# A graph kernel on Trainium2: the sums of the first 32 nodes, instead of 16, from a bf16 matrix of counts

## The chip, the cores and the metric

The kernel runs on one core of a Trainium2 chip. The metric is the device time of one execution in microseconds (us); the median of the runs shown is quoted, and lower is better. Engines are named as in the profile: PE is TensorE's matmul, PEld its weight load, DVE VectorE, ACT ScalarE, POOL GpSimd, SP SyncE. "L516" is line 516 of the kernel before.

## What is computed

There are 6250 nodes with 256 features each and 100,000 edges, each with a source `src`, a destination `dst` and one of 8 types. The edges are sorted by `dst`, and `dst` grows with the square of the edge's place: node 0 has many edges, late nodes have few. Three layers of a relational graph convolution come first, then an attention layer; both have a residual and a layer norm. The part that matters here is the layer:

```python
for l in range(n_layers):                       # 3 layers
    xr = jnp.einsum('nd,rde->rne', x, W_rel[l]) # 8 types
    msg = xr[edge_type, src]
    agg = jax.ops.segment_sum(msg, dst, num_segments=x.shape[0])
    x = jax.nn.relu(agg + x @ W_root[l] + bias[l])
...
x = _layernorm(x + L0(x))
x = _layernorm(x + L1(x))                       # the attention layer
```

All is float32.

## The kernel before

**Sums first, weights later.** For each destination and each type the kernel sums the rows `x[src]` over the edges, and multiplies the sums by the weights of the type afterwards. The 100,000 edges are cut into 782 tiles of 128. An edge tile is handled so: POOL fetches its 128 rows by an indirect DMA (`gather`, L495, one DMA for each tile, L499); DVE makes a 128 x 8W matrix of zeros and ones that tells destination and type of each edge (`onehot`, L479, for four tiles at once, four steps ahead); PE multiplies rows and matrix (`windows`, L504, matmuls L516, two fp32 matmuls for each tile); DVE adds the result, a window of W destinations (3 to 26, growing along the edges), to the sums S in SBUF (`add`, L521, L528). S is a ring of 4 or of 3 node tiles, one ring for the late edges (f = 0, "A") and one for the earlier ones (f = 1, "B").

**Dense work.** When all edges of a node tile are through, `dense` (L577) multiplies its sums by the weights: 16 fp32 matmuls of 256 columns (L586), and two for the root weights (L582). They are handed out in pieces of one matmul, six pieces a step (PIECE), so that they lie between the windows. `finish` (L598) adds the bias on DVE, ACT takes the relu, SP stores the rows for the next layer; ACT clears the ring's columns (`clear`, L594).

**Steps and their order.** `Plan.order()` puts the tiles into groups of four, from the last edges to the first, A and B groups by turns. A layer goes through the 188 groups, one a step, and the code order within a step (L785 to L830) is the order in which every engine's queue gets its instructions: preparation of the attention (last layer, from step PREP_AT = 164), two moves of `counting`, one of `hot`, loads of node rows, the gathers of this step, the onehots of the fourth step ahead, logits, `finish`, the windows, dense pieces, the additions, transposes and folds. All engines take their instructions in order. The order is written out by hand (`tc.manual_schedule`), so nothing is rearranged.

**The first nodes.** The edges of the first nodes are not gathered at all. For HOT = 16 nodes the plan leaves out the first 36 tiles (`TH`). In their place stands a matrix A of counts: how often each source row is used by each pair of one of 16 nodes and one of 8 types, 128 columns for each of the 49 row tiles. `count` (L640) makes it once, in layer 0, from step COUNT_AT = 56: for each pair of node and edge tile, 138 in all, DVE makes a 128 x 392 matrix of zeros and ones in bf16 (L654), and PE multiplies it (L663) with another (L649); ACT copies the result into A, in fp32 (L666). `products` (L670) then computes, in every layer from step HOT_AT = 130, A times the rows: SP loads four row tiles at a time (512 KB) into a buffer "msg", PE multiplies in fp32 (L692), a step later, and DVE adds to `sums` (L697); at the end two transposes bring the sums into S. 13 such loads take 26 steps.

**Buffers.** The gathered groups and the rows for `products` share the pool `mp` of 8 buffers "msg" (L205), used in turn. The PSUM pool `ps_w` has 4 buffers for windows, `ps_d` has 2, for dense results, counts and products; `ps_t` has 1. The pool `hp` (L208), one for all layers, holds the tiles of `count`, `products` and `prepare`.

**A flag.** `tables` counts cases in which the plan's assumptions on the edges don't hold; if there are any, a general kernel runs behind the fast one (L154). It does not run with these inputs.

Of the kernel before, what the change touches and what calls it, by code (L numbers as in the profile page):

```python
# [10 lines left out]
F32 = mybir.dt.float32  # L11
# [9 lines left out]
P = 128  # L21
# [2 lines left out]
NS = (4, 3)  # L24
PAD = 32
MARGIN = 800
HOT = 16
SELS = 6
LOWS = 17
COUNT_AT = 56  # L30
HOT_AT = 130
NEAR = 450
DB = 32
PREP_AT = 164
# [83 lines left out]
@with_exitstack  # L118
def kernel(
    ctx: ExitStack,  # L120
    tc: tile.TileContext,
    x: bass.AP,
    src: bass.AP,
    dst: bass.AP,
    edge_type: bass.AP,
    w_rel: bass.AP,
    w_root: bass.AP,
    bias: bass.AP,
    weight: bass.AP,
    attn_l: bass.AP,  # L130
    attn_r: bass.AP,
    out: bass.AP,
):
# [12 lines left out]
    dram = ctx.enter_context(tc.tile_pool(name="dram", bufs=1, space=DRAM))  # L146
    xs = [x] + [dram.tile([N, D], F32, name=f"x{l}") for l in range(1, L)]

    flag = const.tile([1, 1], I32, name="flag")

    fast(tc, const, pl, x, xs, src, dst, edge_type, w_rel, w_root, bias, weight,
         attn_l, attn_r, out, flag)

    bad = nc.values_load(flag[0:1, 0:1], min_val=0, max_val=6 * T)  # L154
    with tc.If(bad > 0):
        general(tc, x, src, dst, edge_type, w_rel, w_root, bias, weight, attn_l, attn_r, out)


def fast(tc, const, pl, x, xs, src, dst, edge_type, w_rel, w_root, bias, weight,
# [10 lines left out]
    with ExitStack() as top:  # L170
# [14 lines left out]
        yT0 = tab.tile([P, KC, P], F32, name="yT0")  # L185


        A = tab.tile([P, NT, HOT * R], F32, name="A")

        psi = top.enter_context(tc.tile_pool(name="psi", bufs=1, space=PSUM))  # L190
        iota = psi.tile([P, max(R * WMAX, NT * R)], F32, name="iota")
# [10 lines left out]
        with ExitStack() as s:  # L202
# [2 lines left out]
            mp = s.enter_context(tc.tile_pool(name="mp", bufs=8))  # L205
            op = s.enter_context(tc.tile_pool(name="op", bufs=AHEAD + 2))
            xp = s.enter_context(tc.tile_pool(name="xp", bufs=3))
            hp = s.enter_context(tc.tile_pool(name="hp", bufs=1))  # L208
            ps_w = s.enter_context(tc.tile_pool(name="ps_w", bufs=4, space=PSUM))
            ps_d = s.enter_context(tc.tile_pool(name="ps_d", bufs=2, space=PSUM))  # L210
            ps_t = s.enter_context(tc.tile_pool(name="ps_t", bufs=1, space=PSUM))
# [30 lines left out]
            with tc.manual_schedule():  # L242
                for l in range(L):
                    wr, wo = load_w(l)
                    opn = layer(
                        tc, pl, l, l == L - 1, groups, ready, S, hold, A, hk, hl, idx, key, pos,
                        iota, ident, wr, wo, bias_b, x, xs, eps, w1x, altab, y,
                        (al3, ga, hif, yT0, lane, dst, iota_p),
                        mp, op, xp, hp, ps_w, ps_d, ps_t, H)
# [211 lines left out]


def layer(tc, pl, l, final, groups, ready, S, hold, A, hk, hl, idx, key, pos, iota, ident, wr, wo,
          bias_b, x, xs, eps, w1x, altab, y, att, mp, op, xp, hp, ps_w, ps_d, ps_t, H):
    nc = tc.nc
    N, D = x.shape
    KC = D // P
# [172 lines left out]
    def count():  # L640

        lows, made, pc = {}, [], None
        pairs = [(n, t) for n in range(HOT) for t in pl.hot_tiles(n)]
        for m in range(len(pairs) + SELS - 2):
            if m < len(pairs):
# [24 lines left out]
    def products():  # L670

# [26 lines left out]
        pt = ps_t.tile([P, 4 * P], F32, name="pt")  # L698
        for k in range(KC):
            nc.tensor.transpose(pt[:, k * P:(k + 1) * P], sums[:, k * P:(k + 1) * P], ident)  # L700
        for k in range(KC):
            o = cols(1, 0)[:, k * R:(k + 1) * R, :HOT]
            nc.vector.tensor_tensor(
                o, o, pt[:, k * P:k * P + HOT * R].rearrange("p (n r) -> p r n", r=R), ALU.add)
        yield

    al3, ga, hif, yT0, lane, dst, iota_p = att
# [77 lines left out]
    for i in range(NG + 5):  # L785
# [592 lines left out]
```

## Time and profile before

| | |
|---|---|
| median of 3 runs | 2970.67 us (2969.94 to 2975.62) |
| the profiled execution | 2981.72 us, span 2980.0 us |
| granted PE clock, mean | 0.939 |
| PE / PEld busy | 2684.0 us (90%) / 2436.3 us (82%) |
| POOL busy | 2136.6 us (72%) |
| DVE / ACT busy | 1664.3 us (56%) / 452.7 us (15%) |
| gathers (L499) | 2238, 0.95 us each |
| matmul instructions of windows (L516) / dense (L586) | 8952 / 4800 |
| first and last gather begin, layer 0 | 11.3, 945.4 us |
| first and last gather begin, layers 1 and 2 | 964.8, 2866.8 us |

An fp32 matmul shows as two MATMUL instructions. In the groups, the number after the bar is the busy time, then the mean duration in ns of one instruction, which for PE contains the time in the pipeline, so that instructions follow each other faster than their duration. "Idle before" is the time that the engine stood still ahead of them, with what ended it.

### The profile page before, as it was taken

Reading aid. Unit: us, or ns where it says so; the run is one execution under the profiler, and the core shown is the slowest. Engines: PE = TensorE matmul, PEld = TensorE weight load, DVE = VectorE, ACT = ScalarE, POOL = GpSimd, SP = SyncE. Lnnn points to the kernel's source line nnn. Section 1 sums busy time; section 2 is a strip of 40 time slices with the busy share of each in tenths; the row PEclk is TensorE's granted clock in tenths of the full one; section 3 lists DMA queues with packets and bytes.
Section 4 is the critical chain, followed back from the end, with each engine's and each line's share of the span. In section 5 each row is a group of like instructions: output and inputs, shape, how many; then the busy total and the mean of one; then the engine's idle time right before and its main releaser. Section 6 shows DMA issues by size and latency. Waiting matters only on the chain.

```text
span 2980.0 us, 45437 instructions
## 1 busy us (share of the span) xinstructions
PE 2684.0 (90%) x15806; PEld 2436.3 (82%) x15807; DVE 1664.3 (56%) x4097; ACT 452.7 (15%) x599; POOL 2136.6 (72%) x2254
## 2 busy tenths in 40 slices
PE   5999999999877899998988987789999999999985
PEld 4998888888776788988877887678888888888874
DVE  7555677764432555555454443355556655554768
ACT  2111111111001011111111010111111111110114
POOL 6777777777775777777777777577777777777731
PEclk9999999999988899999999997799999999998985
DMA  4444444445433444444444544344444444454534
GB/s 151 122 124 123 122 120 123 120 133 159 146 116 106 129 123 122 124 124 117 123 117 148 163 126 117 118 123 127 130 124 128 124 125 128 136 176 137 167 114 167
DMA packets 203054, 388.99 MB, mean 131 GB/s; under 512 B 42885, under 2 KB 128004, under 8 KB 202820
## 3 DMA queue, kind: packets, MB, share of 16 engines
q0 software_dynamic: 107424, 293.48, 34.2%
q1 hardware_dynamic: 92200, 89.76, 9.4%
q8 instruction: 131, 2.15, 0.3%
q10 hardware_dynamic: 3196, 2.76, 0.3%
q14 instruction: 103, 0.84, 0.1%
HBM read 360.18 MB, written 25.65 MB: 129 GB/s over the span
## 4 chain that ended last, share of the span: by engine, by line
PE 70%; POOL 10%; issue 8%; DVE 6%; DMA 3%; ACT 2%; DVEq 0%; ACTq 0%; POOLq 0%; SPq 0%
PE pw L516 31%; PE pd L586 31%; POOL msg L499 10%; PE pd L582 4%; DMA msg<-x,idx 2%; DVE S L528 2%; PE pd L692 1%; PE pt L560 1%; PE pt L636 1%; ACT xT L563 1%; DMA msg<-in_x_dram,idx 1%; PE pd L663 1%; DVE st L1034 0%; DVE z L1022 0%; PE pw L749 0%
## 5 line engine op out<-in xcount | busy, mean ns | idle before, releaser
L499 POOL DMA_INDIRECT msg<-x,idx x1492 | 1417.2, 950 | 504.3 <-issue 420.2
L516 PE MATMUL pw<-oh,msg 128*128 128x160 f32 (+22 forms) x8952 | 1300.7, 302 | 187.4 <-DMA msg<-x,idx 95.2
L528 DVE TENSOR_TENSOR S<-S,pw 128x320 f32 (+22 forms) x2238 | 904.3, 404 | 989.5 <-PE pd L586 504.3
L516 PEld LDWEIGHTS pw<-oh,msg 128*128 128x128 f32 x8952 | 1245.0, 201 | 253.6 <-issue 109.6
L586 PE MATMUL pd<-wr,S 128*128 128x256 f32 x4800 | 1130.9, 386 | 2.2 <-DVE S L528 1.9
L586 PEld LDWEIGHTS pd<-wr,S 128*128 128x128 f32 x4800 | 913.2, 194 | 122.6 <-DVE S L528 3.9
L499 POOL DMA_INDIRECT msg<-in_x_dram,idx x746 | 708.0, 949 | 236.4 <-issue 209.7
L483 DVE TENSOR_TENSOR oh<-iota,key 128x640 f32<-128x640 f32 (+23 forms) x564 | 363.9, 647 | 25.6 <-issue 13.9
L595 ACT ACTIVATE S<-S 128x2048 uint32<-128x2048 uint32 x150 | 285.0, 1900 | 25.9 <-PE pd L586 25.9
L563 ACT COPY xT<-pt 128x256 f32<-128x256 f32 x195 | 72.4, 371 | 1048.1 <-PE pt L560 1046.7
L609 ACT ACTIVATE h<-pd 128x256 f32<-128x256 f32 x98 | 37.7, 385 | 903.3 <-DVE pd L606 669.0
L582 PE MATMUL pd<-wo,xT 128*128 128x256 f32 x588 | 167.8, 411 | 3.2 <-ACT h L609 3.2
L606 DVE TENSOR_TENSOR pd<-pd,bias_b 128x256 f32<-128x256 f32 x147 | 63.2, 430 | 186.6 <-PE pd L586 186.4
L582 PEld LDWEIGHTS pd<-wo,xT 128*128 128x128 f32 x588 | 109.3, 203 | 12.9 <-ACT h L609 3.6
L654 DVE TENSOR_SCALAR sel<-iota,hk 128x392 bf16<-128x392 f32 x138 | 80.4, 613 | 0.0
L619 ACT ACTIVATE rs<-mv,eps 128x1 f32<-128x1 f32 x49 | 14.4, 295 | 403.8 <-DVE mv L618 403.8
L692 PE MATMUL pd<-msg,A 128*128 128x256 f32 x294 | 71.9, 387 | 1.9 <-DMA msg<-x 1.9
L692 PEld LDWEIGHTS pd<-msg,A 128*128 128x128 f32 x294 | 55.6, 196 | 9.1 <-issue 2.2
L560 PE MATMUL pt<-ident,xin 128*128 128x128 f32 x294 | 58.3, 281 | 1.4 <-ACT xT L563 1.4
L636 PEld LDWEIGHTS pt<-w1x,xT 128*128 128x128 f32 x192 | 26.6, 201 | 35.3 <-ACT xT L563 35.3
L560 PEld LDWEIGHTS pt<-ident,xin 128*128 128x128 f32 x294 | 41.8, 147 | 13.2 <-ACT xT L563 2.8
L636 PE MATMUL pt<-w1x,xT 128*128 128x4 f32 x192 | 30.8, 266 | 23.6 <-ACT xT L563 23.6
(187 smaller groups left out, 629.3 us busy)
## 6 DMA issues: line engine op xcount, KB each, us to landing
msg<-x,idx POOLq DMA_INDIRECT x1492, 2.8
x<-h SPq DMA_DIRECT2D x96, 128.0 KB
xin<-x SPq DMA_DIRECT2D x96, 128.0 KB
msg<-x SPq DMA_DIRECT2D x24, 512.0 KB
msg<-in_x_dram,idx POOLq DMA_INDIRECT x746, 2.8
y<-yt SPq DMA_DIRECT2D x49, 128.0 KB
xin<-in_x_dram SPq DMA_DIRECT2D x48, 128.0 KB
msg<-in_x_dram SPq DMA_DIRECT2D x12, 512.0 KB
```

What stands on the lines that cost most here:

```text
L483: nc.vector.tensor_tensor(oh[:, :len(g), :w], iota[:, :w].unsqueeze(1).to_broadcast([P, len(g), w]), key[:, g[0]:g[-1] + 1].unsqueeze(2).t ...
L499: nc.gpsimd.indirect_dma_start(out=msg[:, q, :], out_offset=None, in_=table, in_offset=bass.IndirectOffsetOnAxis(ap=idx[:, t:t + 1], axis=0))
L516: nc.tensor.matmul(pw[:, k * w:(k + 1) * w], msg[:, q, k * P:(k + 1) * P], oh[:, q, :w], start=True, stop=True)
L528: ins = nc.vector.tensor_tensor(o, o, pw.rearrange("p (a b) -> p a b", b=W), ALU.add)
L560: nc.tensor.transpose(pt[:, k * P:(k + 1) * P], t[:, k * P:(k + 1) * P], ident)
L563: nc.scalar.copy(xT.rearrange("p k n -> p (k n)"), pt[:, :D])
L582: nc.tensor.matmul(pd[:, :D], xT[:, k], wo[:, k], start=(k == 0), stop=False)
L586: i = nc.tensor.matmul(pd[:, :D], s[:, k * R + r], wr[:, k, r], start=(xT is None and k == r == 0), stop=(k == KC - 1 and r == R - 1))
L595: i = nc.scalar.memzero(cols(f, j))
L636: nc.tensor.matmul(pt[:, :H], yT[:, k], w1x[:, k, D + H:D + 2 * H], start=(k == 0), stop=(k == KC - 1))
L654: nc.vector.tensor_scalar(oh, iota[:, :NT * R], float(512 * n), hk[:, t:t + 1], op0=ALU.add, op1=ALU.is_equal)
L692: nc.tensor.matmul(ph[:, :D], A[:, j], t[:, n], start=(n == 0), stop=(j == js[-1]))
```

## The change

HOT becomes 32, so the plan leaves out 52 tiles instead of 36 and a layer has 184 groups instead of 188; there are 272 pairs of node and edge tile instead of 138. A has 256 columns for each row tile, in bf16, which takes as many bytes as before. Counts up to 256 are exact in bf16; a new check takes the largest count and raises the flag if it is over 256. Counting begins at step 8 instead of 56. `products` begins at step 148 in layer 0 and 130 in the others. It loads one load further ahead, splits the fp32 rows into three bf16 parts whose sum is exact (ACT copies the first, DVE subtracts it in place, ACT copies the second, and in the next step DVE makes the third), and multiplies each of them with both halves of A: six bf16 matmuls for each row tile instead of one in fp32. The sums have two halves of 256 columns. The pool `hp` is made anew for each layer.

```diff
-HOT = 16
+HOT = 32
...
-COUNT_AT = 56
-HOT_AT = 130
+COUNT_AT = 8
+HOT_AT = 148, 130
...
-    bad = nc.values_load(flag[0:1, 0:1], min_val=0, max_val=6 * T)
+    bad = nc.values_load(flag[0:1, 0:1], min_val=0, max_val=6 * T + P)
...
-        A = tab.tile([P, NT, HOT * R], F32, name="A")
+        A = tab.tile([P, NT, HOT * R], BF16, name="A")
...
-            hp = s.enter_context(tc.tile_pool(name="hp", bufs=1))
...
-                    opn = layer(
...
+                    with tc.tile_pool(name=f"hp{l}", bufs=1) as hp:
+                        opn = layer(
...
     def count():
         lows, made, pc = {}, [], None
+        top = hp.tile([P, HOT], F32, name="top")
...
                 if t == tiles[-1]:
                     nc.scalar.copy(A[:, :, n * R:(n + 1) * R],
                                    pc[:, :NT * R].rearrange("p (j r) -> p j r", r=R))
+                    nc.vector.tensor_reduce(top[:, n:n + 1], pc[:, :NT * R], AX.X, ALU.max)
             yield
+
+        most = hp.tile([P, 2], F32, name="most")
+        nc.vector.tensor_reduce(most[:, 0:1], top, AX.X, ALU.max)
+        nc.vector.tensor_scalar(most[:, 0:1], most[:, 0:1], 256.5, None, op0=ALU.is_gt)
+        nc.vector.memset(most[:, 1:2], 1.0)
+        pt = ps_t.tile([P, 4 * P], F32, name="pt")
+        nc.tensor.matmul(pt[0:1, 0:1], most[:, 0:1], most[:, 1:2], start=True, stop=True)
+        nc.vector.tensor_copy(most[0:1, 0:1], flag)
+        nc.vector.tensor_tensor(most[0:1, 0:1], most[0:1, 0:1], pt[0:1, 0:1], ALU.add)
+        nc.vector.tensor_copy(flag, most[0:1, 0:1])
+        yield
...
-        sums = hp.tile([P, D], F32, name="sums")
-        for js in loads:
-            t = load(js)
+        HH = HOT * R // P
+        HN = HOT // HH
+        sums = hp.tile([P, HH * D], F32, name="sums")
+        x3 = hp.tile([P, 3, GT * D], BF16, name="x3")
+        rows_of, ph, m = {0: load(loads[0])}, None, 0
+        yield
+        for m, js in enumerate(loads):
+
+            if m + 1 < len(loads):
+                rows_of[m + 1] = load(loads[m + 1])
+            w = len(js) * D
+            t = rows_of.pop(m).rearrange("p a d -> p (a d)")[:, :w]
+            nc.scalar.copy(x3[:, 0, :w], t)
+            nc.vector.tensor_tensor(t, t, x3[:, 0, :w], ALU.subtract)
+            nc.scalar.copy(x3[:, 1, :w], t)
             yield
+            nc.vector.tensor_tensor(x3[:, 2, :w], t, x3[:, 1, :w], ALU.subtract)
             ph = ps_d.tile([P, 512], F32, name="pd")
-            for n, j in enumerate(js):
-                nc.tensor.matmul(ph[:, :D], A[:, j], t[:, n], start=(n == 0), stop=(j == js[-1]))
+            for h in range(HH):
+                for n, j in enumerate(js):
+                    for c in range(3):
+                        nc.tensor.matmul(ph[:, h * D:(h + 1) * D], A[:, j, h * P:(h + 1) * P],
+                                         x3[:, c, n * D:(n + 1) * D], start=(n == c == 0),
+                                         stop=(j == js[-1] and c == 2))
             yield
-            if js[0] == 0:
-                nc.vector.tensor_copy(sums, ph[:, :D])
+            if m == 0:
+                nc.vector.tensor_copy(sums, ph[:, :HH * D])
             else:
-                nc.vector.tensor_tensor(sums, sums, ph[:, :D], ALU.add)
+                nc.vector.tensor_tensor(sums, sums, ph[:, :HH * D], ALU.add)
...
-        if i >= HOT_AT:
+        if i >= HOT_AT[min(l, 1)]:
             next(hot, None)
...
-    v = A.rearrange("p j s -> p (j s)").bitcast(BF16)
+    v = A.rearrange("p j s -> p (j s)")
```

Four transposes instead of two, and four additions instead of two, bring the sums into S at the end of `products`.

More of the change, by code (lines that the diff above doesn't have):

```diff
@@ L244, in fast @@
                     wr, wo = load_w(l)
-                    opn = layer(
[L246 to L249, printed above, removed]
+                    with tc.tile_pool(name=f"hp{l}", bufs=1) as hp:
+                        opn = layer(
+                            tc, pl, l, l == L - 1, groups, ready, S, hold, A, hk, hl, idx, key, pos,
+                            iota, ident, wr, wo, bias_b, x, xs, eps, w1x, altab, y,
+                            (al3, ga, hif, yT0, lane, dst, iota_p), flag,
+                            mp, op, xp, hp, ps_w, ps_d, ps_t, H)
         with tc.manual_schedule():
@@ L463, in layer @@
 def layer(tc, pl, l, final, groups, ready, S, hold, A, hk, hl, idx, key, pos, iota, ident, wr, wo,
-          bias_b, x, xs, eps, w1x, altab, y, att, mp, op, xp, hp, ps_w, ps_d, ps_t, H):
+          bias_b, x, xs, eps, w1x, altab, y, att, flag, mp, op, xp, hp, ps_w, ps_d, ps_t, H):
     nc = tc.nc
@@ L693, in products @@
             yield
-            if js[0] == 0:
-                nc.vector.tensor_copy(sums, ph[:, :D])
+            if m == 0:
+                nc.vector.tensor_copy(sums, ph[:, :HH * D])
             else:
-                nc.vector.tensor_tensor(sums, sums, ph[:, :D], ALU.add)
+                nc.vector.tensor_tensor(sums, sums, ph[:, :HH * D], ALU.add)
         pt = ps_t.tile([P, 4 * P], F32, name="pt")
+        for h in range(HH):
+            for k in range(KC):
+                nc.tensor.transpose(pt[:, (h * KC + k) * P:(h * KC + k + 1) * P],
+                                    sums[:, h * D + k * P:h * D + (k + 1) * P], ident)
@@ L699, in products @@
         for k in range(KC):
[L700 to L704, printed above, removed]
+            for h in range(HH):
+                o = cols(1, 0)[:, k * R:(k + 1) * R, h * HN:(h + 1) * HN]
+                q = (h * KC + k) * P
+                nc.vector.tensor_tensor(
+                    o, o, pt[:, q:q + P].rearrange("p (n r) -> p r n", r=R), ALU.add)
```

## Prediction

> **What bounds the kernel now.** I read the chain of waits first, then the costliest groups, then busy time by stretch, then the waits of POOL and VectorE, and last the timeline inside single steps.
>
> ```profile
> PE 70%; POOL 10%; issue 8%; DVE 6%; DMA 3%; ACT 2%; DVEq 0%; ACTq 0%; POOLq 0%; SPq 0%
> L499 POOL DMA_INDIRECT msg<-x,idx x1492 | 1417.2, 950 | 504.3 <-issue 420.2
> ```
>
> The chain names PE, but POOL is as full: a gather is busy 0.95 us and followed by 0.30 us of "issue", 1.25 us in all, and 746 of them per layer make 934 us of a layer's some 950. So two engines run side by side with nearly equal loads. Busy time by stretch, one for each layer (stretch, then PE, PEld, DVE, ACT, POOL, clock, DMA):
>
> ```profile
> 40.00:350.00 310.00, 296.07 (x1702) 271.37 (x1702) 180.63 (x363) 55.53 (x59) 234.73 (x248) 0.98 0.43 126
> 990.00:1280.00 290.00, 279.96 (x1614) 256.56 (x1613) 157.78 (x311) 45.58 (x53) 219.53 (x232) 0.99 0.42 122
> 2000.00:2270.00 270.00, 256.93 (x1500) 232.66 (x1499) 163.59 (x370) 48.17 (x68) 200.53 (x212) 0.99 0.44 128
> ```
>
> 310 us hold 248 gathers (1.25 us each): POOL never stops in layers 0 and 1. In layer 2 it is 212 in 270 us (1.27): there it waits.
>
> To see who leads I paired, in the timeline, the 4 gathers of each step with its 16 matmuls of L516, and took as **lag** the time from the end of the step's last gather to its first matmul. At least 1.9 us of it is the landing. Layer 0: 14.7 at step 8, 23.7 at step 56, 28.2 at step 80, 5.8 at 128, then 2 to 8. Layer 1: 1.9 at step 8, 11.7 at 44, 1.9 at 130, 9.3 at 140, 6.1 at the end. Layer 2: 3.8, 30.4 at 44, 38.0 at 60, 20.0 at 130, 18.0 at the end, never back at the floor. So layers 0 and 1 end with POOL as the bound, and layer 2 is PE's from step 12 on. 38 us is where 8 msg buffers are full and POOL has to wait for PE.
>
> ```profile
> POOL msg L499 <- PE pw L516: 43.3, 108, 3.5
> DVE S L528 <- PE pd L586: 504.3, 105, 7.7
> DVE S L528 <- PE pw L516: 375.6, 296, 8.9
> ```
>
> The second line matters below: in 105 of the some 560 steps the additions into S (L528) cannot start when the windows are done, but only when PE has ended that step's dense matmuls, which read S. One such step in the timeline (start, duration, what, and in brackets the idle time before it):
>
> ```profile
> 2662.92 2.75 PE L586 MATMUL pd<-wr,S 128*128 128x256 f32 x12
> 2665.71 1.92 DVE L528 TENSOR_TENSOR S<-S,pw 128x288 f32 x4 [4.50 <-PE pd L586]
> ```
>
> DVE stands idle for 4.5 us, and starts its four additions when the 12 dense matmuls are over.
>
> [...] For 392 columns [...] the trace has 165 (a pair of L663 takes 0.33 us to the next instruction). For 256 columns [...] I use 0.11 us. [...] the trace has 693 ns for 512 columns at L569[...]. [...] the gathers around it mostly keep 1.25 us, a few are up to 0.4 us late. The new subtractions are of that kind too, 78 of them: 0 to 15 us of POOL time, 0 taken, because POOL waits in that phase anyway.
>
> **The change part by part.** Unit times: a 256-column fp32 matmul instruction 0.219 us (12 in 2.63 on the chain; each fp32 matmul is two instructions), a window instruction 0.128 below 128 columns, 0.15 to 0.17 above (16 in 2.71 at 208), a count 0.165. I went through the steps in the order of the plan and summed windows, dense pieces, transposes, counts and products of each stretch. That reproduces what is seen where PE has no lack of data: layer 0, steps 8 to 56, 254 us worked out, 250 seen (66.6 to 316.2 us).
>
> *Gathers removed.* Tiles 0 to 35 are left out now; the limit for 32 nodes gives 52. 16 gathers per layer at 1.25 us are **-20 us** of POOL per layer, -60 in all. PE loses 16 x 4 x 0.128 = -8.2 us per layer. Groups fall from 188 to 184 a layer, while dense work stays, so it is packed 2% tighter.
>
> *Counting, layer 0.* Pairs of node and tile go from 138 to 272: +134 x 0.165 = +22 us PE, +134 x 0.613 (L654) = +82 us DVE, and they start at step 8 instead of 56, exactly where PE is 96% busy. PE work for steps 8 to 56 becomes 266 us (250 seen + 96 x 0.165) against POOL's 48 x 5.006 = 240: lag 14.7 + 26 = 40, over the limit of 38; POOL waits 2. Steps 56 to 80: 126 against 120, 6 more. Then PE is faster (80 to 148: 314 against 340), lag about 9 at step 148. The 32 new maxima make DVE wait for PE's counts ahead of its own onehots, and the pd buffer held by a count is now held among denser dense work; nothing before shows this: 0 to 15 us (half a microsecond for each maximum), I take 5, since in steps 56 to 127 the same pd sharing shows no excess over the sum. The final flag chain, the memset and the copies: one small chain, 0 to 2, in the 5.
>
> *Products.* Per row tile 6 bf16 matmuls x 0.11 instead of 2 instructions x 0.219: 147 x 0.22 = +32 us PE, 10.8 per layer. ACT gets 26 copies of 1024 columns per layer (about 0.97 us each from L595, 1900 ns for 2048), hidden: ACT is 15% busy. DVE gets 26 subtractions x 1.22 and additions of 512 columns instead of 256: some +35 us per layer, hidden as load (DVE is 45% busy there) but **not as a chain**. Today PE's products wait for a load alone. Then the 24 matmuls of a product wait for the third part, a subtraction that DVE makes after the previous step's additions. If that step had dense work without conflict, DVE is through in its shade: 0. If it had none (13 of the 28 steps, since five dense tiles fall due there and each takes three), PE stands for the last addition and the subtraction: about 1.6 us. If the additions waited for the dense part (19%): four additions, say 1.7, + 1.22 + 0.2 = 3.1. Mean 0.46 x 1.6 + 0.19 x 3.1 = **1.33 us per product, 17 per layer**. Bounds 0 and 3.1; below nothing is excluded, because PE's own work per product grows too.
>
> *The msg buffers.* A product's rows also take one of the 8. Today PE frees them one step after the load; then they are loaded one step earlier and freed by DVE three steps after. Every second step's gather must then wait for work of the step but two before it: three steps of 5.0 less 4.0 (windows, last addition, subtraction) and less the 4.9 of its own gathers leave a lag of at most 6 us in these 28 steps. A hint from before: in layer 2 the lag falls from 20 to 13 in the product phase, with POOL waits of up to 2 us.
>
> Sums for the product phase (28 steps, POOL 140.2): PE 137 in layer 0 and 139 in layer 1, 154 and 156 with the chain.
> Layer 0: POOL -20 + 2 + 6 + 3 (lag 9 pressed to 6) + 14 + 5 = **+10**.
> Layer 1: -20 + (156 - 140 - 4 of lag that is free) = **-8**.
> Layer 2, PE's: -8.2 + 10.8 + 17, four steps' small stalls -1.6, and the preparation, whose last two rounds fall behind the last gather instead of one, +2: **+20**. Its 20 us of POOL only lengthen a wait.
> Total +22. The profiled execution took 2981.7 (span 2980.0), so 3003.7 against it; the runs' median is 2970.67, 0.4% lower, and I forecast **2993**.
>
> **Rivals.** *A, faster: DVE is always ahead, the products cost matmuls alone.* Layer 0: -20 + 2 + 6 + 3 = -9, layer 1: -20 (139 fits into 140), layer 2: +3. That is -26: 2945. For it: DVE is only half busy; against it, the 504 us of L528. The break-even is at 0.75 us of chain per product (39 x 0.75 = 29): below that the kernel is faster. Chance 0.17. *B, no change*: 0.6 to 0.9 us per product, 2971. Chance 0.14. *C, much slower*: every product pays the long wait of 3.1 us, 40 a layer: layer 0 -20 + 11 + 37 + 5 = +33, layer 1 -20 + 39 - 4 = +15, layer 2 +3 + 40 = +43; 3062. Dense work in the half of the steps that hides the chain speaks against it. Chance 0.10. *D, gathers bound everything*: -60, 2911; the lag in layer 2 speaks against it. Chance 0.03. The forecast, up to 3015: 0.56.
>
> About 0.2%, 6 us, is what a measurement can tell from no change. Faster 0.20 (A and D), same 0.14, slower 0.66. The range 2945 to 3035 leaves out D, part of A and most of C.
>
> **What would show it.** In the profile after: 2190 gathers; 272 counts; bf16 products of 256 columns at 0.11 us; PE waiting on DVE's third part, some 1.3 us each; POOL waiting for PE in layer 0 before step 80 and in every product phase; first gathers of layers 1 and 2 some 10 us late and 2 us late. I am wrong if PE's wait for the third part is below 0.75 us, if POOL runs on at 1.25 us through the product phases, or if layer 2 shortens with its gathers.

## The result, and the profile after

The changed kernel takes **3087.78 us** (median of 4 runs, 3083.85 to 3089.36) against 2971.5 us for the kernel before in the same rounds: a ratio of 1.0387, 95% interval 1.0369 to 1.0405. The forecast was slower, by 22 us; it is slower by 116. The profiled execution has a span of 3086.5 us (before: 2980.0) and a mean granted clock of 0.936 (0.939).

The chain of waits of this run breaks off after a tenth of the span, so I lean on the groups, the waits and the stretches instead. First some of the costliest groups of the changed kernel:

```profile
L499 POOL DMA_INDIRECT msg<-x,idx x1460 | 1407.1, 964 | 573.2 <-issue 411.1
L720 PE MATMUL pd<-x,A 128*128 128x256 bf16 x882 | 137.8, 317 | 75.0 <-DVE x L715 61.3
L664 PE MATMUL pd<-sel,low 128*128 128x392 bf16 x272 | 69.2, 331 | 18.6 <-DVE top L669 18.6
L711 ACT CAST x<-msg 128x1024 bf16<-128x1024 f32 (+1 forms) x39 | 38.8, 996 | 173.0 <-PE pd L720 103.6
L713 ACT CAST x<-msg 128x1024 bf16<-128x1024 f32 (+1 forms) x39 | 38.8, 996 | 153.9 <-DVE msg L712 153.9
```

The gathers and counts are as many as forecast (1460 + 730, and 272). The products L720 stand idle for 75 us, 61 of it for the third part L715. The last line is one that the forecast did not think of: ScalarE's second cast L713 waits 154 us in all for VectorE's subtraction L712, and what stands behind the cast on ScalarE waits with it: a copy (L563) in the last timeline of this section has its input at 2654.46 us and begins at 2660.93, behind both casts. Then the waits (engine, line and releaser: us in total, times, longest):

```profile
PE pd L720 <- DVE x L715: 61.3, 35, 4.3
PE pt L636 <- ACT xT L563: 39.8, 48, 6.9
PE pd L664 <- DVE top L669: 18.6, 9, 3.1
POOL msg L499 <- PE pw L516: 146.3, 141, 11.4
```

Before, the second of them was:

```profile
PE pt L636 <- ACT xT L563: 23.6, 48, 0.5
```

It is PE waiting for ScalarE's copy xT (L563) in front of the logits (the attention layer's scores of the nodes, made in layer 2). None of these waits was over 0.5 us before; now single ones last 6.9 us. POOL waits 146 us for buffers that PE still holds, where it waited 43 before.

Where in the span does this stand? Busy time by stretch (stretch and length in us, then PE, PEld, DVE, ACT, POOL busy with their instructions, granted clock, DMA share, GB/s), cut at the first window matmuls of steps. Before: layer 0, steps 8 to 148; then 28 steps with products in layers 0 (148 to 176; there the older plan is near its end of products), 1 and 2 (130 to 158 in both):

```profile
66.60:758.60 692.00, 667.62 (x4004) 605.30 (x4003) 433.14 (x950) 110.25 (x137) 523.76 (x553) 1.00 0.44 129
758.60:897.50 138.90, 116.51 (x679) 106.45 (x678) 56.08 (x149) 12.54 (x15) 105.09 (x111) 0.86 0.41 121
1618.40:1762.30 143.90, 131.15 (x767) 119.69 (x768) 62.74 (x162) 14.43 (x18) 108.85 (x116) 0.92 0.51 153
2599.00:2738.70 139.70, 131.37 (x798) 119.80 (x796) 71.86 (x195) 15.71 (x23) 103.75 (x110) 0.95 0.51 156
```

After, the same steps:

```profile
67.80:799.10 731.30, 693.17 (x4092) 617.01 (x4090) 517.62 (x1124) 118.87 (x155) 531.20 (x562) 0.98 0.40 116
799.10:969.50 170.40, 139.15 (x942) 121.73 (x942) 90.65 (x196) 39.70 (x43) 120.22 (x113) 0.89 0.46 135
1668.00:1839.40 171.40, 142.81 (x949) 127.00 (x950) 92.53 (x191) 37.85 (x41) 125.20 (x119) 0.91 0.46 136
2652.20:2860.30 208.10, 163.04 (x985) 141.80 (x986) 103.61 (x226) 40.47 (x49) 115.47 (x113) 0.84 0.39 115
```

Two places lengthen: the counting of layer 0 (+39 us) and the product phases, above all that of layer 2 (140 to 208 us), where the clock falls from 0.95 to 0.84. By first gathers, layers last 998.9, 957.9 and 1118.2 us (with the end) instead of 953.5, 954.2 and 1061.0: **+45, +4, +57**, where +10, -8, +20 were forecast.

In layer 2's product phase the timeline of PE shows it step by step (start, duration, what, and in brackets the idle time before it):

```profile
2684.40 4.11 PE L720 MATMUL pd<-x,A 128*128 128x256 bf16 x22 [2.93 <-DVE x L715]
...
2699.65 3.83 PE L720 MATMUL pd<-x,A 128*128 128x256 bf16 x22 [4.25 <-DVE x L715]
...
2709.56 1.01 PE L636 MATMUL pt<-w1x,xT 128*128 128x4 f32 x4 [3.23 <-ACT xT L563]
```

PE stands for 2.9, 4.3 and 3.2 us within 26 us, and what follows a wait is slow: 22 products take 4.11 us, 0.187 each. In the run without subtractions, below, 24 of them take 2.78 us, 0.116 each:

```profile
2632.10 2.78 PE L717 MATMUL pd<-x,A 128*128 128x256 bf16 x24
```

The granted clock (the third figure from the end) in slices of 1 us behind the first of these waits of the changed kernel:

```profile
2684.00:2685.00 1.00, 0.60 (x6) 0.54 (x6) 0.65 (x2) 0.00 (x0) 0.38 (x1) 1.00 0.45 131
2685.00:2686.00 1.00, 1.00 (x8) 0.72 (x7) 0.00 (x0) 0.00 (x0) 0.69 (x2) 0.61 0.00 0
2686.00:2687.00 1.00, 1.00 (x6) 0.69 (x5) 0.00 (x0) 0.00 (x0) 0.81 (x1) 0.50 0.42 131
2687.00:2688.00 1.00, 1.00 (x7) 0.71 (x5) 0.00 (x0) 0.00 (x0) 0.88 (x1) 0.50 0.40 119
2688.00:2689.00 1.00, 1.00 (x9) 0.93 (x7) 0.00 (x0) 0.84 (x1) 0.69 (x2) 0.69 0.29 66
2689.00:2690.00 1.00, 1.00 (x12) 1.00 (x10) 0.00 (x0) 0.20 (x1) 0.32 (x1) 1.00 0.20 78
```

It is halved for some 3.4 us, and then full again. So this wait on VectorE is paid once as 2.93 us of idle time and once more as a lower clock.

ScalarE's part in the longest wait for a logits copy (6.88 us, at the start of layer 2's product phase) is this:

```profile
2657.64 1.04 ACT L711 CAST x<-msg 128x1024 bf16<-128x1024 f32 x1 [4.40 <-DMA msg<-x]
2659.97 1.04 ACT L713 CAST x<-msg 128x1024 bf16<-128x1024 f32 x1 [1.29 <-DVE msg L712]
2660.93 0.37 ACT L563 COPY xT<-pt 128x256 f32<-128x256 f32 x1
```

The copy stands behind both casts: PE's transpose L560, its input, has ended at 2654.46 us, 6.47 us before the copy begins. The first cast waited 4.40 us for the load of its rows, the second 1.29 us for the subtraction.

### The profile page after: what moved, and what is told of

It reads as the page before. It is cut to its first block, busy times and chain, and to the rows that moved or that the text cites. A ratio compares the mean times of both kernels' runs of the same rounds, so it can differ in the third digit from the quotient of the medians.

```text
span 3086.5 us, 46868 instructions
## 1 busy us (share of the span) xinstructions
PE 2735.4 (89%) x16344; PEld 2451.6 (79%) x16345; DVE 1826.6 (59%) x4309; ACT 535.9 (17%) x693; POOL 2125.4 (69%) x2206
## 5 line engine op out<-in xcount | busy, mean ns | idle before, releaser
L528 DVE TENSOR_TENSOR S<-S,pw 128x320 f32 (+21 forms) x2190 | 893.7, 408 | 936.2 <-PE pd L586 464.0
L516 PE MATMUL pw<-oh,msg 128*128 128x184 f32 (+22 forms) x8760 | 1263.0, 300 | 132.8 <-DMA msg<-x,idx 77.7
L516 PEld LDWEIGHTS pw<-oh,msg 128*128 128x128 f32 x8760 | 1204.8, 199 | 218.1 <-issue 88.1
L483 DVE TENSOR_TENSOR oh<-iota,key 128x416 f32<-128x416 f32 (+22 forms) x552 | 359.9, 654 | 17.3 <-issue 7.5
L563 ACT COPY xT<-pt 128x256 f32<-128x256 f32 x195 | 72.4, 371 | 1087.9 <-PE pt L560 1087.9
L720 PE MATMUL pd<-x,A 128*128 128x256 bf16 x882 | 137.8, 317 | 75.0 <-DVE x L715 61.3
L720 PEld LDWEIGHTS <-A 128*128 128x128 bf16 x882 | 99.6, 113 | 107.7 <-issue 83.3
L582 PE MATMUL pd<-wo,xT 128*128 128x256 f32 x588 | 166.6, 408 | 9.1 <-ACT h L609 6.1
L655 DVE TENSOR_SCALAR sel<-iota,hk 128x392 bf16<-128x392 f32 x272 | 158.7, 614 | 0.0
L609 ACT ACTIVATE h<-pd 128x256 f32<-128x256 f32 x98 | 37.7, 384 | 620.4 <-DVE pd L606 477.8
L582 PEld LDWEIGHTS pd<-wo,xT 128*128 128x128 f32 x588 | 108.3, 201 | 21.0 <-ACT h L609 8.6
L664 PE MATMUL pd<-sel,low 128*128 128x392 bf16 x272 | 69.2, 331 | 18.6 <-DVE top L669 18.6
L711 ACT CAST x<-msg 128x1024 bf16<-128x1024 f32 (+1 forms) x39 | 38.8, 996 | 173.0 <-PE pd L720 103.6
L636 PE MATMUL pt<-w1x,xT 128*128 128x4 f32 x192 | 31.0, 267 | 39.8 <-ACT xT L563 39.8
L713 ACT CAST x<-msg 128x1024 bf16<-128x1024 f32 (+1 forms) x39 | 38.8, 996 | 153.9 <-DVE msg L712 153.9
```

The source lines that it names most:

```text
L483: nc.vector.tensor_tensor(oh[:, :len(g), :w], iota[:, :w].unsqueeze(1).to_broadcast([P, len(g), w]), key[:, g[0]:g[-1] + 1].unsqueeze(2).t ...
L516: nc.tensor.matmul(pw[:, k * w:(k + 1) * w], msg[:, q, k * P:(k + 1) * P], oh[:, q, :w], start=True, stop=True)
L528: ins = nc.vector.tensor_tensor(o, o, pw.rearrange("p (a b) -> p a b", b=W), ALU.add)
L563: nc.scalar.copy(xT.rearrange("p k n -> p (k n)"), pt[:, :D])
L582: nc.tensor.matmul(pd[:, :D], xT[:, k], wo[:, k], start=(k == 0), stop=False)
L655: nc.vector.tensor_scalar(oh, iota[:, :NT * R], float(512 * n), hk[:, t:t + 1], op0=ALU.add, op1=ALU.is_equal)
```

## The experiments

Three theories were held against each other. **W**: PE waits in line behind the third part and ScalarE's casts, and its clock falls in the waits. **P**: the added matmuls are the cost. **G**: VectorE's two-input subtractions hold up POOL's gathers.

On some of the chips that the experiments ran on, the kernel before itself took some 3590 to 3630 us instead of 2971, with added stalls on every engine whose cause I don't know, so runs are compared as ratios to the kernel before on their own chip, and sums in microseconds that the expectations give against 2971 us are read that way.

### The mark and the three runs that decide

These four ran on one chip, where the kernel before takes 2975.47 us (2966.92 to 2980.67, 18 runs), like the first.

**The changed kernel again.**

> The changed kernel again, as the mark for the three runs beside it: 1.030 of the kernel before if the chip is like the last one (1.0301 there), 1.039 if it is like the first.

3081.62 us, ratio 1.0363 (1.0343 to 1.0384): 106 us slower than before. Its span is 3085.8.

**No subtractions.** The edit:

```diff
...
             nc.scalar.copy(x3[:, 0, :w], t)
-            nc.vector.tensor_tensor(t, t, x3[:, 0, :w], ALU.subtract)
-            nc.scalar.copy(x3[:, 1, :w], t)
             yield
-            nc.vector.tensor_tensor(x3[:, 2, :w], t, x3[:, 1, :w], ALU.subtract)
...
-                                         x3[:, c, n * D:(n + 1) * D], start=(n == c == 0),
+                                         x3[:, 0, n * D:(n + 1) * D], start=(n == c == 0),
```

> Leaves out both subtractions and the second cast: the first bf16 part is multiplied three times, so that the sums lose precision; every matmul stays. P (the added matmuls) expects the time of the changed kernel within 0.3%. W (TensorE waits for the parts, ScalarE's casts hold up the logits, the clock falls) and G (subtractions hold up gathers) expect most of the change's cost gone: 1.002 to 1.010 of the kernel before.

(The first part multiplied three times also makes the sums about three times too large.) **2962.14 us**, ratio 0.9966 (0.9953 to 0.9979): 119 us less than the changed kernel, and even 13 less than the kernel before, where W and G expected a little more than it takes (1.002 to 1.010). All 882 product matmuls and all counts are still there, so P is out. The three product phases of this run:

```profile
800.20:933.10 132.90, 127.64 (x943) 116.42 (x943) 64.07 (x169) 26.91 (x30) 100.17 (x106) 0.97 0.56 166
1629.80:1769.60 139.80, 133.93 (x949) 123.17 (x949) 66.37 (x165) 25.32 (x28) 105.72 (x112) 0.94 0.54 161
2588.50:2738.40 149.90, 139.29 (x985) 127.25 (x986) 77.03 (x200) 27.61 (x36) 103.53 (x110) 0.94 0.53 156
```

Held against the same three lines of the changed kernel, they split the loss. PE executes as many instructions (943, 949, 985 against 942, 949, 985). The phases are shorter by 37.5, 31.6 and 58.2 us, 127.3 in all, of a difference of 128.7 between the spans: nearly all of what separates the two runs is lost here (the counting in layer 0 takes 732 us in both). Of it, PE's busy time is 11.5 + 8.9 + 23.8 = **44 us**: the same instructions at a lower clock. The clock records of both traces know two values, 1.0 and 0.5. In the three phases PE is busy at 0.5 for 110 us in the changed kernel and for 31 in this run, and half of the difference, 39 us, is most of the 44. The rest of the loss, **83 us**, is PE standing still. The waits name it: 61.3 for the third part, 11.4 for the second cast, and 11 more for the logits' copies than this run has (39.8 against 28.6), 84 together.

**Subtractions that nobody waits for.** Both casts read the loaded rows, the parts made by VectorE go to a tile of their own, and the matmuls read the first part only:

```diff
...
-            nc.scalar.copy(x3[:, 0, :w], t)
-            nc.vector.tensor_tensor(t, t, x3[:, 0, :w], ALU.subtract)
-            nc.scalar.copy(x3[:, 1, :w], t)
+            nc.scalar.copy(x3[:, :w], t)
+            nc.scalar.copy(y3[:, 0, :w], t)
+            nc.vector.tensor_tensor(t, t, x3[:, :w], ALU.subtract)
             yield
-            nc.vector.tensor_tensor(x3[:, 2, :w], t, x3[:, 1, :w], ALU.subtract)
+            nc.vector.tensor_tensor(y3[:, 1, :w], t, y3[:, 0, :w], ALU.subtract)
...
-                                         x3[:, c, n * D:(n + 1) * D], start=(n == c == 0),
+                                         x3[:, n * D:(n + 1) * D], start=(n == c == 0),
...
```

> Keeps both subtractions and both casts, with their sizes, but nobody waits for the subtractions: both casts read the loaded rows, and the matmuls multiply the first part three times (the sums lose precision). W expects the time of the run without subtractions, within 0.4%: the waits are gone. G expects the time of the changed kernel, since the subtractions still stand beside the gathers. Half way between would mean that both count.

**3000.68 us**, ratio 1.0094 (1.0075 to 1.0112): 81 us of the 119 are gone with the waits alone, so W holds for two thirds. But 38 us stay, and neither W nor G alone allows that. They go with the gathers: summed over the trace, gathers of more than 1 us are 40.5 us longer than the usual 0.946 (15.2, 14.7 and 10.6 us in the three layers), against 5.3 us in the run without subtractions. The layers are longer by 19, 14 and 10 us, and in the product phases PE waits 17 us for gathered rows against 6. The next run's timeline shows how a gather is held up. (The two ways of dividing the 119 us overlap. In the changed kernel the longer gathers add up to as much, but POOL also stands 146 us for PE there, against 101 here; that they mostly vanish in this standing is inferred, not shown.)

**The waits moved away, no work left out.** The third part is made ahead of the interruption, so that a step's windows stand between it and its matmuls; and the products' step is issued behind the logits, so that their copies stand ahead of the casts on ScalarE.

```diff
-            yield
             nc.vector.tensor_tensor(x3[:, 2, :w], t, x3[:, 1, :w], ALU.subtract)
+            yield
...
-        if i >= HOT_AT[min(l, 1)]:
-            next(hot, None)
...
         log = [(k, t) for k, t in log if k > i - 2]
+        if i >= HOT_AT[min(l, 1)]:
+            next(hot, None)
```

> Same computation as the changed kernel, no work left out: the third part is made ahead of the interruption, and the products' step is issued after the logits of its step, so that the logits' copies stand ahead of the casts on ScalarE. W expects 40 to 70 us off the changed kernel (1.012 to 1.020 of the kernel before) and no wait of TensorE over 2 us for the third part or for a logits copy behind a cast. P and G expect the changed kernel's time within 0.3%.

**3015.43 us**, ratio 1.0145 (1.0123 to 1.0166): 66 us off the changed kernel, as W expects; P and G expected nothing. Its waits for the same two things (the third part is made in L714 here):

```profile
PE pd L720 <- DVE x L714: 25.1, 29, 1.0
PE pt L636 <- ACT xT L563: 24.6, 48, 1.4
```

The logits are back at their 24 us, and the third part's wait is down to 1.0 at most. (18 us of waits for the casts remain.) PE is busy at half the clock for 60 us of the three phases instead of 110 (57 in the run above). Layer 2's product phase lasts 168 us instead of 208, at a clock of 0.92:

```profile
2621.10:2789.00 167.90, 148.12 (x984) 129.82 (x985) 106.17 (x226) 40.58 (x49) 117.80 (x118) 0.92 0.49 145
```

Two places in the timeline of this run, with VectorE's subtraction and POOL's gather side by side:

```profile
2640.05 1.22 DVE L712 TENSOR_TENSOR msg<-msg,x 128x1024 f32<-128x1024 f32 x1
2640.10 1.99 POOL L499 DMA_INDIRECT msg<-x,idx  x1 [0.30 <-issue]
...
2651.55 1.22 DVE L712 TENSOR_TENSOR msg<-msg,x 128x1024 f32<-128x1024 f32 x1
2651.65 1.94 POOL L499 DMA_INDIRECT msg<-x,idx  x1 [0.30 <-issue]
2653.89 0.95 POOL L499 DMA_INDIRECT msg<-x,idx  x1 [0.31 <-issue]
```

A gather that begins 0.05 or 0.10 us after the subtraction takes 1.99 or 1.94 us and not 0.95: longer by about as much as the subtraction had left to run. The next one is at 0.95 again. In the changed kernel's trace 47 gathers begin inside a subtraction with more than 0.2 us of it left. Every one of them takes over 1 us, and ends 0.81 to 0.83 us after the subtraction. The onehots (L483) are the counter-test: they too have two inputs, but one of them, `iota`, lies in PSUM. Some 150 gathers begin inside a onehot with as much of it left and meet no subtraction and no L569, and none takes more than 0.95 us.

### Each move alone

These ran on chips where the kernel before took 3590 to 3630 us, most of them without the changed kernel beside them on the same chip. Ratios carry over from chip to chip only roughly: the run without subtractions is at 1.0046 in this part and was at 0.9966 above. So a difference of less than about 0.01 between chips decides nothing here, and the waits in the traces carry the argument. First the mark, and the kernel before for its trace:

> The changed kernel itself, unedited, on a chip like those of the other experiments, where the kernel before took about 3590 us and not 2971. Theories W (TensorE waits in line behind the third part and the casts, and its clock falls in these waits), P (the added matmuls themselves) and G (the subtractions hold up the gathers) all expect a ratio near 1.039 on a chip where the kernel before takes 2971 us. Where it takes 3590 us, the same microseconds added (116) would give 1.032; if the slower surroundings already hide part of the waits, less, down to about 1.015.

> The kernel before, unedited, for its trace on this chip: 2971 us if the chip is like the first, about 3590 us if it is like those of the other experiments. In the second case its trace should show where the 620 us stand: in gathers of more than 1.25 us, in a lower clock, or in stalls of all engines together.

3738.46 us against 3629.91, ratio 1.0301 (1.0251 to 1.0351): 108 us slower, nearly the same microseconds. The kernel before took 3647.53 in its one run here; PE, VectorE and ScalarE all stand still together for 417 us of it and not 81, while the distance from one gather to the next is at its usual 1.25 us in the median. What brings these stalls is not known.

The third part ahead of the interruption (the first hunk above):

> The third part is made ahead of the interruption of the products' step instead of after it, so that a step's windows stand between it and the matmuls that read it. Work on every engine is the same. W: TensorE's waits for the third part (61 us in the changed kernel) go to under 10 us, the clock of the product phases rises, and the time falls by 30 to 60 us against the changed kernel on the same chip (ratio to it 0.98 to 0.99). P and G: within 0.3% of the changed kernel, since no matmul and no subtraction goes.

3722.02 us, 1.0230 (1.0177 to 1.0283), on the mark's chip. The intervals overlap, so the time alone shows no gain. PE's idle time ahead of L720 falls from 104.6 to 50.7 us and the wait for the third part from 62.7 to 18.0 (W expected under 10); the logits' waits stay nearly what they were (62.5 and 56.8), and those for the second cast go from 20.3 to 29.4.

The products' step behind the logits (the second hunk), run twice:

> The changed kernel with the step of the products issued after the logits, so that the logits' transposed copies on ScalarE (layer 2) no longer stand behind casts that wait for VectorE; the rest as in the changed kernel. Theory W: the 19 us of waits and some 10 of clock in layer 2 go, the waits for the third part stay or grow a little, since VectorE's onehots now stand ahead of it: about 3060 us. Theory P: 3087.

> Only the products' step after the logits of its step; the third part stays after the interruption. Same computation. W: the waits for the logits' copies fall to the 25 us of the kernel before and the time by 25 to 45 us (1.021 to 1.028 of the kernel before, against 1.036 for the changed kernel and 1.0145 with both moves); the waits for the third part stay. P and G: the changed kernel's time.

The first is one run: 3654.05 against 3587.8. The second: 3657.23 us, 1.0186 (1.0158 to 1.0214). That is a little less time than W expected (1.021 to 1.028). Against the mark the logits' waits fall from 62.5 us to 38.8 (45.0 in the single run), and the waits for the third part **rise** from 62.7 to 94.8 (106.3), as is to be expected where the later step leaves VectorE less time ahead of the products. So this move alone buys part of its gain with the other's wait; both together, above, leave 25 us of each.

The third part's matmuls last, also run twice:

```diff
-            for h in range(HH):
-                for n, j in enumerate(js):
-                    for c in range(3):
+            for c in range(3):
+                for h in range(HH):
+                    for n, j in enumerate(js):
...
```

> The changed kernel, with the loop over the three parts outside: 16 matmuls with the first two parts (1.8 us) come before the 8 that need the third. All work and all subtractions stay. Theory W: most of the 61 us of waits for the third part is covered, and a part of the clock comes back; the logits' wait for ScalarE stays: about 3010 us. Theory P: 3085. Theory G: 3085, since the subtractions stay.

> The changed kernel with the loop over the three parts outside, once more, on a chip whose time of the kernel before can be set against the 2971 us. 16 matmuls with the first two parts come before the 8 that need the third. Theory W (PE waits behind VectorE's third part and ScalarE's casts, and its clock falls in these waits): 0.975 of the changed kernel's time, 3010 us where the kernel before takes 2971. Theory P (the added work itself) and theory G (the subtractions hold up the gathers): 3085.

3661.31 us, 1.0169 (1.0117 to 1.0221), where W expected about 1.013 and P and G the mark's time, and 3661.14 against 3587.8 in the one run of the second. The wait for the third part goes to 32.3 and 37.7 us, not to nothing: the 16 matmuls ahead of it last some 2 us, and the wait was up to 5.9 in the mark.

The run without subtractions here, for the first time:

> The changed kernel, but the products use the first bf16 part three times: the second cast and both subtractions are left out (so the sums of the first nodes are less exact), the number of matmuls, loads and gathers stays. Theory W (PE waits in line behind VectorE's third part and behind ScalarE's casts, and its clock falls in these waits): the 61 us of waits for the third part, the 19 us of waits for the logits' transposes in layer 2 and some 20 us of lowered clock go: about 2985 us. Theory P (the products' and counts' own PE work is larger than thought): that work is the same, so at least 3070. Theory G (the subtractions hold up the gathers on POOL, 43 us in all): up to 43 us less, about 3050.

3618.98 us, 1.0046 (1.0015 to 1.0077): near the kernel before, as on the other chip, though a little above it and not below.

### The other parts

**The removed gathers alone**, in the kernel before, with nothing in their place (16 more tiles of edges per layer are missing from the sums):

```diff
-    while self.hot_high(self.TH) < HOT - 0.01
+    while self.hot_high(self.TH) < 32 - 0.01
...
-        return [t for t in range(self.TH)
+        return [t for t in range(36)
```

> The kernel before with 52 tiles left out instead of 36 (the gathers, windows and additions of tiles 36 to 51 are left out and nothing stands for them; counting and products are as before, for the first 36 tiles). It measures the gain alone. POOL as the bound of layers 0 and 1: -20 us each, in layer 2 the 8 us of PE's windows: 2925 us. If the gathers bind everything: -60, 2911. If PE binds everything: -25, 2946.

3534.28 us in one run, against 3587.8 in one: 53.5 us for 48 gathers, 1.1 us each. The kernel before spreads over some 30 us on such chips, so the size is rough; but the gain that was the point of the change is there.

**The split alone**: the counts for 16 nodes as before, in bf16, the products in three parts, no maxima.

```diff
-HOT = 32
+HOT = 16
...
-COUNT_AT = 8
-HOT_AT = 148, 130
+COUNT_AT = 56
+HOT_AT = 130, 130
...
```

> The kernel before (16 nodes, 36 tiles left out, counting from step 56, products from step 130, no maxima), with the products alone changed: rows split into three bf16 parts, three bf16 matmuls for each row tile. PE has 0.33 us of work for each row tile instead of 0.44. Theory W: 13 waits of 1.5 us per layer, the logits' waits and the clock, less 16 us of work, and a part that POOL's lead covers in layers 0 and 1: about 3020 us. Theory P: 2971 or a little less, since PE has less to do. Theory G: about 2990.

3643.75 us, 1.0098 (1.0067 to 1.0128): 35 to 42 us lost to the split (by the ratio and by the medians) with no gather removed. W expected some 49, G some 19 and P none.

**No maxima of the counts**, no flag made of them, run twice:

```diff
...
-                    nc.vector.tensor_reduce(top[:, n:n + 1], pc[:, :NT * R], AX.X, ALU.max)
...
```

> The changed kernel without the 32 maxima of the counts and without the check that uses them (the flag for counts over 256 is left out). Theory W: the 19 us in which the next count waits for its PSUM buffer, held by a maximum on VectorE, go, with a little clock: about 3066 us. Rival: these waits lie where POOL or the dense matmuls would have stopped PE anyway: 3087.

> The changed kernel without the maxima of the counts and without the flag made of them (leaves the check for counts above 256 out). The maxima sit in the first layer alone, where 18.6 us of waits of TensorE name them: 10 to 25 us off the changed kernel, all in the first layer (1.028 to 1.033 of the kernel before, where the changed one is at 1.036). No change within 0.2% would mean that the first layer's step times are set by the counting itself.

3649.82 us, 1.0127 (1.0089 to 1.0164), and 3657.37 us, 1.0169 (1.0138 to 1.0200). Against the mark's 1.0301 from another chip that would be 47 to 63 us, some three times what 18.6 us of named waits allow. The place where the maxima stand doesn't show so much: layer 0's steps 8 to 148 take 842, 856 and 842 us in three runs without them (the third is the next one), and 851 to 873 in six runs with them on chips of about the same speed, 14 us more in the mean. The rest I can't place; the price of the maxima stays open between some 14 and 60 us.

**All three together**: third matmuls last, products behind the logits, no maxima.

> The changed kernel with three edits: the third part's matmuls last, the step of the products issued after the logits instead of ahead of the gathers, and no maxima (the check of counts over 256 is left out). Theory W: all its named waits are gone or covered; left are 32 + 22 us of PE work, of which layers 0 and 1 hide a part, against 60 us of gathers: 2965 us, about as before. Theory P: above 3060. Theory G: above 3050.

3645.62 against 3587.8 in one run, 1.6% above the kernel before where W expected about its time, and no better than the maxima left out alone. PE's wait for the third part is 81 us there: behind the logits, matmul order does not hide it.

**Two parts**: one cast, one subtraction that writes the second part, products behind the logits.

```diff
             nc.scalar.copy(x3[:, 0, :w], t)
-            nc.vector.tensor_tensor(t, t, x3[:, 0, :w], ALU.subtract)
-            nc.scalar.copy(x3[:, 1, :w], t)
+            nc.vector.tensor_tensor(x3[:, 1, :w], t, x3[:, 0, :w], ALU.subtract)
             yield
-            nc.vector.tensor_tensor(x3[:, 2, :w], t, x3[:, 1, :w], ALU.subtract)
...
-                    for c in range(3):
+                    for c in range(2):
...
```

> Two bf16 parts instead of three, and the products' step after the logits: one cast, one subtraction that writes the second part, 588 matmuls instead of 882; leaves out the third part, so the sums of the first 32 nodes keep about 16 bits of the rows instead of all 24. W: no second cast stands behind a subtraction on ScalarE, so no logits copy waits, but the subtraction's wait of about a microsecond may stay at each product: about 2975 us where the kernel before takes 2975 (0.995 to 1.005 of it). G and P expect half of the subtractions and a third of the matmuls to bring back a third to a half of 106 us: 1.018 to 1.024.

3588.63 us against 3592.48, ratio **0.9992** (0.9963 to 1.0021): no difference from the kernel before, as W expected, and only 5.3 us of PE's waits for a part are left. But the logits' waits are at 53.4 us and not at the 24.7 of the kernel before on such a chip, which W did not expect, and a third of the product matmuls is gone as well. It is the quickest variant here that still splits the rows, and it does not beat the kernel before.

## Why the prediction was wrong

The direction was right, the reason half right, and the size off by a factor of five. By its own steps:

*Gathers removed: right.* 2190 gathers, and 53.5 us less (one run) when nothing else is changed, against -60.

*The sum without the chain: nearly right.* Rival A, the forecast without PE's waits, was -26. The run without subtractions is at -13 by medians and -22 by the profiled spans, and its layers stand at +9, -23 and -9 against the kernel before where A had -9, -20 and +3. So gathers, counts and matmuls were priced well as a total, with some luck: the errors of layers 0 and 2 go against each other.

*Counting: the work right, the wait too small.* PE's busy time in steps 8 to 148 rises by 25.6 us against 22. But "the 32 new maxima make DVE wait" was taken as 5, bounds 0 to 15; PE's waits named after the maxima are 20.6 us there (18.6 at the counts and 2.0 at L582). The 0.5 us that set the upper bound for each maximum was too small: the longest wait is 3.1 us.

*The third part's chain: right as a wait.* 17 us per layer were forecast, 17.9, 20.1 and 23.3 measured; 1.57 us per product where 1.33 were taken. The 1.22 us for a subtraction of 1024 columns was an estimate; in the changed kernel's trace L712 and L715 take 1215 and 1213 ns in the mean.

*"ACT gets 26 copies ..., hidden: ACT is 15% busy": the step that failed first.* It counted ScalarE's load and not its order. The second cast waits on ScalarE for a subtraction, and PE waits 11.4 us for that cast itself; the logits' copies stand behind both casts. Of the 39.8 us that PE waits for the copies, 19.0 are in layer 2's product phase, in 6 waits. 7.8 of these are there in the run without subtractions too, behind the one cast that is left; 11.2 belong to the subtraction and the second cast. That is the mistake that the prediction avoided for VectorE ("hidden as load but not as a chain") and made for the next engine.

*Waits were priced as idle time only.* The clock that they cost appears in no term. It is 44 us over the three phases by the comparison above, more than two thirds of the third part's waits. The unit price of 0.11 us per product was an estimate (165 ns for a count of 392 columns, in the trace before, would make it 0.108 for 256 columns if the time went with the columns). It is nearly met where PE does not wait (0.116); after a wait of 2.9 us a product takes 0.187.

*Subtractions against gathers: "0 to 15 us of POOL time, 0 taken, because POOL waits in that phase anyway".* In the changed kernel the reason stands, since POOL waits 146 us for PE; but the size does not: some 40 us of longer gathers in its trace, 35 of them beside the subtractions, against the 15 that were estimated as the most. The kernel before held a better estimate. There L569, 39 operations of 0.69 us with two SBUF inputs, makes gathers 4 us longer in all. Twice as many operations of 1.22 us, with the square of the length if a longer one is met more often and has more left in proportion, would give about 25. And as soon as the waits go, it counts: 38 us between the two runs that differ by the subtractions and ScalarE's second cast. That these 38 are all the gathers' is argued from two sums that agree (35 us more of longer gathers), not shown: VectorE has 78 operations more in that run and ScalarE 39, and no run lengthened gathers by other means.

*"a lag of at most 6 us": wrong.* In the product phases the lag is 13 to 25 us in layer 0, 11 to 25 in layer 1 from step 140 on and 15 to 33 in layer 2. The msg buffers do not press POOL that close to PE.

*Together.* +22 as forecast, +41 for waits (84 measured against the 43, 14 + 12 + 17, that its sum took), +44 of clock, +15 for the maxima, -12 in layer 2's sum: 110, where 106 us stand between the profiled spans. It is an account from sums of the traces and not a measurement of each item. Rival C came nearest in time (3062), but for a reason that did not occur: its long wait at every product. The wait for the third part had nearly the forecast's size; the waits behind the casts and the clock that all of them drag along were missing.

## What to carry to other kernels

An engine that is 15% busy hides nothing by itself: before a new instruction is called hidden, write down what it waits for and what stands behind it on its own engine, and price both waits. A wait that PE did not have before can cost more than its length where PE is the bound, since the matmuls behind it may run at a lower clock; here 44 us of a lower clock came with 83 us of waits. Where a chain over two engines feeds PE, shorten the chain or put a whole step of other work between its end and its reader, and look at all of its readers: putting the products behind the logits alone shortened one wait and lengthened the other.

## What the runs showed of the hardware beyond that

A VectorE subtraction of 1.22 us with both inputs in SBUF can double a gather that begins just after its start, from 0.95 to 1.99 us, and 78 of them made 35 us of longer gathers; a comparison with one of its two inputs in PSUM made none (some 150 gathers, none over 0.95 us). TensorE's clock fell to half, for some 3.4 us, after a wait of 2.93 us. The run without subtractions, at 2962 us, has the same matmuls as the changed kernel at 3082, so that a difference of 4% in the whole span came from operations on two engines that were 59% and 17% busy.
